# Layer norms as ScalarE activations, retention's moments on VectorE, and a planner that lists single operations

## The chip, the cores and the metric

The kernel runs on one core of a Trainium2 chip. A core has five engines with a queue of instructions each: TensorE (PE) for matrix products, VectorE (DVE), ScalarE (ACT) and GpSimd (POOL) for elementwise work, and SyncE (SP), which here only starts DMAs. SBUF holds the working data in 128 partitions; PSUM takes the results of PE, in banks of 128x512 float32. The metric is device time in microseconds (us).

## The reference, cut to what matters

The input `x` is 4 sequences of 512 tokens with 128 features. Eight sublayers follow each other, each as `x = x + f(layernorm(x))`. The layer norm has no weights:

```python
def _layernorm(x, axis=-1, eps=1e-05):
    m = jnp.mean(x, axis=axis, keepdims=True)
    v = jnp.var(x, axis=axis, keepdims=True)
    return (x - m) / jnp.sqrt(v + eps)
```

The sublayers are, in order: softmax attention with 16 heads of 8; a mixture of 8 experts, top 2; Favor+ linear attention; the experts again; a gated linear attention with 8 heads of 64, which has a layer norm of its own on the normed input and adds that input back (`residual`); a feed-forward of width 352 whose activations and weights are rounded to FP4 in blocks of 16; retention with 16 heads of 8; and the feed-forward again. Retention ends in a norm over all 512 tokens and the 8 features of a head:

```python
mean = y.mean(axis=(1, 3), keepdims=True)      # y: (batch, head, token, feature)
var = y.var(axis=(1, 3), keepdims=True)
y = (y - mean) * jax.lax.rsqrt(var + GN_EPS)
y = y.reshape(B, T, C) * gn_w + gn_b
```

## The kernel before, in words

All of `x` stays in SBUF as `X`, 16 tiles of 128 tokens by 128 features; a batch (one sequence) is four tiles. A norm of a batch has three parts. `moments` (L265) lets DVE take mean and variance of each tile (`bn_stats`, `bn_aggr`). `rstd` (L249) computes 1/sqrt by an integer first guess on DVE and three Newton steps, twelve small operations on POOL (L259 to L262). `centred` (L272) then writes `xn = (X - mean) * r` in four POOL operations of 128x128, one per tile, at L275. PE transposes the four tiles into one PSUM bank (L309) and ACT copies that out (`transposed`, L303). Every sublayer's norm goes this way except attention's: there `norm` (L284) takes the moments of all 16 tiles first, does one `rstd` of 128x16 for all four batches, and its four operations per batch are at L298. There are 36 such groups of four: 4 in attention, 8 in the experts (a unit q is one batch in one of the two expert layers), 4 in Favor+, 4 in the gates of the gated attention and 4 for its residual `res` (L984), and 4 in each of the two feed-forwards and in retention.

The program has four stretches. First X is loaded, attention's batch 0 is normed and projected, and 32 DMAs (SP, 16 for `qc` and 16 for `kc`, L363) spread the heads over the padded tiles `qpad` and `kpad`. Then comes attention, a pipeline over 16 units of four heads: scores (L385 takes maxima), exponentials (L410), values. Then one loop over 64 pairs of a unit q and an expert e, whose order is written out by hand; Favor+ and the gates (`gates`, L826) are generators that move one step at a time between the experts' matmuls. A unit's norm, transposes and routing are placed some steps ahead of its first expert. In an expert, POOL multiplies `h` (L584) and DVE finishes it (L585).

The last stretch, which I call the tail, is `rest` (L1267): five streams per batch, as Python generators. `gated` is the gated attention in chunks (`chunked`, L1005), `first` the first feed-forward, `retention` its matmuls, `leveled` its norm and output projection, `second` the second feed-forward, which stores the batch. The class `Clock` (L126) is a planner that runs while the program is built: each stream yields at the places where PE would have to wait, with an estimated due time; `steps` goes on with the stream that can start earliest, and of equals with the one whose number is higher (gated 150 to 270, first 150, retention 110, leveled 75, second 50). Two feed-forwards may be open at a time and one retention. PE's queue has this order exactly; the other engines' queues come from a scheduler and the places where instructions were issued. PSUM has four slots `bank` of one bank and two slots `pair` of two there, which this planner doesn't count.

In a feed-forward, `fp4_pieces` (L1213) rounds by block: DVE takes block maxima (L1217 to L1220), POOL multiplies by the reciprocal scale (L1225), DVE rounds (`fw`), POOL multiplies back (L1235). The four `gates` products go through ACT's silu (L1312) and a DVE product into KD (L1313); `down` rounds half of the result and, tile by tile, transposes it (L1332), copies it to `hT` on ACT (L1334) and multiplies. In retention, the scores of a group G of four heads go through DVE's `copy_predicated` into `rw` (L1395) and through ACT and POOL (L1397). `values` and `leveled` then read:

```python
nc.scalar.activation(y[:, G, :], po, AF.Copy, accum_out=sums[:, G:G + 1])        # L1426
self.mm(ps, k["avg"], sums)                       # mean over a head, by a matmul
nc.vector.tensor_scalar(gm, ps, -1.0, None, ALU.mult)                            # L1451
nc.scalar.activation(off, y[:, G, :], AF.Square, bias=gm[:, G:G + 1], accum_out=gv[:, G:G + 1])   # L1454
self.mm(ps, k["avg"], gv)                         # variance
nc.scalar.activation(y[:, G, :], y[:, G, :], AF.Identity, scale=ga[:, G:G + 1], bias=gm[:, G:G + 1])  # L1463
```

Of the kernel before, what the change touches and what calls it, by code (L numbers as in the profile page):

```python
# [17 lines left out]
P = 128  # L18
# [12 lines left out]
def _constants():  # L31
# [28 lines left out]
    c["avg"] = np.where((g[:, None] == g[None, :]) & (d[:, None] < DH), 1.0 / (DH * T), 0.0)  # L60
# [64 lines left out]
class Clock:  # L125


    def __init__(self):
        self.free, self.since = collections.defaultdict(float), 0.0
# [5 lines left out]
    def pe(self, us):  # L135
        return self.run("pe", 1.1 * us, self.since)

    def dve(self, us, since):
        return self.run("dve", 1.1 * us, since)

    def act(self, us, since):
        return self.run("act", us, since)

    def pool(self, us, since):
        return self.run("pool", us, since)

    def together(self, work):

        while work:
            a = min(work, key=lambda a: a[0])  # L150
            yield a[0]
            t = next(a[1], None)
            if t is None:
                work.remove(a)
            else:
                a[0] = t or self.free["pe"]

    def steps(self, streams):

        left = {name: [0.0, after, takes, None, gen, far] for name, (after, takes, gen, far) in streams.items()}
        rooms = {"ffn": 2, "retention": 1}
        while left:
            can = []
            for name, a in left.items():
                if a[3] is None:
                    if any(n in left for n in a[1]) or rooms.get(a[2], 1) == 0:
                        continue
                can.append((max(a[0], self.free["pe"]), -a[5], a[0], name))  # L170
            ready, name = min(can)[2:]
            a = left[name]
            self.since = ready
            if a[3] is None:
                a[3] = a[4]()
                if a[2]:
                    rooms[a[2]] -= 1
            t = next(a[3], None)
            if t is None:
                del left[name]  # L180
                if a[2]:
                    rooms[a[2]] += 1
                for other in left.values():
                    if name in other[1]:
                        other[0] = max(other[0], ready)
            else:
                a[0] = t or self.free["pe"]


class Net:  # L190
# [81 lines left out]
    def centred(self, pool, b, mv, r, tag="xn"):  # L272
        xn = self.new(pool, [P, J, P], tag)
        for j in range(J):
            self.nc.gpsimd.tensor_scalar(xn[:, j, :], self.xi(b * J + j), mv[:, j, 0:1], r[:, j:j + 1], ALU.subtract, ALU.mult)  # L275
        return xn

    def normed(self, pool, b, tag="xn"):

        mv = self.new(self.stat, [P, J, 2], "mvb")  # L280
        self.moments(b, mv)
        return self.centred(pool, b, mv, self.rstd(mv[:, :, 1], "rstdb"), tag)

    def norm(self, src):  # L284

        nc = self.nc
        mv = self.new(self.stat, [P, NT, 2], "mv")
        for i in range(NT):
            st = self.new(self.stat, [P, 6], "bn", bufs=4)
            nc.vector.bn_stats(st, src(i))  # L290
            nc.vector.bn_aggr(mv[:, i, :], st)
        r = self.rstd(mv[:, :, 1], "rstd")

        def make(pool, b, tag):
            xn = self.new(pool, [P, J, P], tag)
            for j in range(J):
                i = b * J + j
                nc.gpsimd.tensor_scalar(xn[:, j, :], src(i), mv[:, i, 0:1], r[:, i:i + 1], ALU.subtract, ALU.mult)  # L298
            return xn

        return make

    def transposed(self, pool, xn, tag, scale=None, bias=None, banks=None):  # L303

        nc = self.nc
        out = self.new(pool, [P, T], tag)
        ps = self.bank(pool=banks)
        for j in range(J):
            nc.tensor.transpose(ps[:, j * P:(j + 1) * P], xn[:, j, :], self.ident)  # L309
        if scale is None:  # L310
            nc.scalar.copy(out, ps)
        else:
            nc.scalar.activation(out, ps, AF.Identity, scale=scale, bias=bias)
        return out
# [12 lines left out]
    def attention(self, beside=None):  # L327
# [9 lines left out]
        with ExitStack() as ctx:  # L337
            tp = lambda name, bufs: ctx.enter_context(self.tc.tile_pool(name="a_" + name, bufs=bufs))
            big, mid, pt = tp("big", 1), tp("mid", 2), tp("pt", 3)
            norm = self.norm(self.xi)  # L340
# [14 lines left out]
            def prepare(b):  # L355
                xs = self.transposed(mid, norm(mid, b, "xn"), "xnT")
# [411 lines left out]
    def front(self, out):  # L768
# [6 lines left out]
        with ExitStack() as ctx, ExitStack() as now:  # L775
# [50 lines left out]
            def gates(b, mid, banks=None):  # L826
# [10 lines left out]
                xn = self.centred(mid, b, mv[:, b], r2[:, b])  # L837
# [146 lines left out]
            def project(b, pool, ot):  # L984
                res = self.centred(pool, b, mv[:, b], r1[:, b], "res")
# [19 lines left out]
    def chunked(self, arm, tp, clock, D, KD, fall, same, tri, wq, wv, rn, xs, project):  # L1005
# [13 lines left out]
        def queries(u):  # L1019
# [3 lines left out]
            tt(D[b][:, p, :], ps, D[b][:, p, :], ALU.mult)  # L1023

        def by_token(u):
# [7 lines left out]
            tt(split(V[u]), split(ps), _bc(rn[:, b, :, p, :], DI), ALU.mult)  # L1033

        def keys(u):
# [5 lines left out]
            nc.scalar.copy(K[u], ps)  # L1041

        def states(u):
# [6 lines left out]
            for c in range(J - 1):  # L1050
                f = fall[:, b, p, c:c + 1]
                stt(r[:, c, :], ps[:, c, :], f, same, ALU.mult, ALU.mult)
                if c:
                    stt(r[:, c, :], r[:, c - 1, :], f, r[:, c, :], ALU.mult, ALU.add)

        def scores(u):
# [6 lines left out]
            nc.vector.copy_predicated(flat(ws[u % 3]), _over(tri, 2 * J), ps.rearrange("p h c t -> p (h c) t"))  # L1063

        def values(u):
# [8 lines left out]
            nc.scalar.copy(D[b][:, p, :], po)  # L1074

        def before(u):

            queries(u)
            ready[u] = clock.dve(0.7, clock.pe(0.85))
            yield 0  # L1080
            by_token(u)
            t = clock.dve(0.7, clock.pe(0.85))
            yield 0
            keys(u)
            yield max(t, clock.act(0.5, clock.pe(0.35)))
            states(u)
            ready[u] = max(ready[u], clock.dve(1.7, clock.pe(0.65)))

        ready = {}

        def steps(b):
            if b == 0:
                yield from before(0)
            for u in range(NG * b, NG * (b + 1)):
                yield ready[u]
                scores(u)
                t = clock.dve(1.3, clock.pe(0.9))
                yield 0
                if u + 1 < NG * B:
                    yield from before(u + 1)  # L1100
                yield t
                values(u)
                t = clock.act(0.6, clock.pe(1.6))
            yield t
            ps = project(b, once, D[b])
            yield clock.pe(3.5)
            self.add_x(b, ps)
            yield clock.dve(0.7, clock.since)
# [158 lines left out]
    def rest(self, arm, clock, D, KD, out, gated=None):  # L1267
# [18 lines left out]
        for t in (S, va, *ws):  # L1286
            nc.gpsimd.memset(t, 0.0)

        def ffn(b, store=False):
            h, hq = room(KD[b])[:, :J * FF], room(D[b])[:, :J * FF]  # L1290
            scale = lambda n: [self.new(two, [P, n // BLK], f"{t}{n}") for t in ("sc", "rc")]
            pe, dve, act, pool = clock.pe, clock.dve, clock.act, clock.pool
            xn = self.normed(two, b).rearrange("p j d -> p (j d)")
            yield pool(4.5, dve(1.6, clock.since))
            fp4 = self.fp4_pieces(xn, xn, *scale(T), self.new(two, [P, T], "fw"))
            next(fp4), next(fp4)
            yield pool(1.1, dve(1.3, clock.since))
            for _ in fp4:
                pass
            yield pool(1.3, dve(2.2, clock.since))  # L1300
            xT = self.transposed(two, xn.rearrange("p (j d) -> p j d", d=P), "xT")
            yield act(0.6, pe(0.45))
            half = J * FF // 2
            po = []

            def gates():
                for j in range(J):
                    ps = self.pair()
                    for i in range(2):
                        self.mm(ps[:, i, :FF], xT[:, chunks[j]], wT[:, i * FF:(i + 1) * FF])  # L1310
                    o = h[:, j * FF:(j + 1) * FF]
                    nc.scalar.activation(o, ps[:, 0, :FF], AF.Silu)  # L1312
                    tt(o, o, ps[:, 1, :FF], ALU.mult)  # L1313
                    t = dve(0.5, act(0.5, pe(1.2)))
                    if j % 2:
                        work.append([t, down(j // 2)])
                    yield 0

            def down(i):
                c = slice(i * half, (i + 1) * half)  # L1320
                fp4 = self.fp4_pieces(hq[:, c], h[:, c], *scale(half), self.new(two, [P, half], "fh"))
                next(fp4), next(fp4)
                yield pool(1.4, dve(1.5, clock.since))
                for _ in fp4:
                    pass
                yield pool(1.4, dve(2.8, clock.since))
                po[:] = po or [self.bank()]
                for j in (2 * i, 2 * i + 1):
                    ps = self.bank()
                    for c in range(NF):  # L1330
                        w = min(P, FF - c * P)
# [178 lines left out]
```

## Time and profile before

| | |
|---|---|
| median of 3 runs | 1328.7 us (1327.78 to 1331.3) |
| the profiled execution | 1344.16 us, of which the span of its instructions is 1342.3 |
| busy in the span | PE 80%, DVE 52%, POOL 40%, ACT 33% |
| mean granted clock of PE | 0.855 |
| first score matmul of attention | 39.1 us |
| experts and Favor+ begin | about 392 us |
| the tail | 894 to 1340 us |

A line of groups in the profile reads: source line, engine, operation, out<-in, shapes, count, then busy time in all and mean ns of one, then the idle time of the engine just before such instructions and who ended it. A line of waits reads: who waited, at which line, for which engine's output, then us in total, times, and the longest. The row of digits is the busy share in 40 equal slices of the span, in tenths.

### The profile page before, as it was taken

Reading aid. Unit: us, or ns where it says so; the run is one execution under the profiler, and the core shown is the slowest. Engines: PE = TensorE matmul, PEld = TensorE weight load, DVE = VectorE, ACT = ScalarE, POOL = GpSimd, SP = SyncE. Lnnn points to the kernel's source line nnn. Section 1 sums busy time; section 2 is a strip of 40 time slices with the busy share of each in tenths; the row PEclk is TensorE's granted clock in tenths of the full one; section 3 lists DMA queues with packets and bytes.
Section 4 is the critical chain, followed back from the end, with each engine's and each line's share of the span. In section 5 each row is a group of like instructions: output and inputs, shape, how many; then the busy total and the mean of one; then the engine's idle time right before and its main releaser. Section 6 shows DMA issues by size and latency. Waiting matters only on the chain.

```text
span 1342.3 us, 17500 instructions
## 1 busy us (share of the span) xinstructions
PE 1074.0 (80%) x6608; PEld 648.4 (48%) x6608; DVE 692.7 (52%) x1607; ACT 445.2 (33%) x738; POOL 534.5 (40%) x1038
## 2 busy tenths in 40 slices
PE   2799898999999999898978877489778857667745
PEld 1444444444345546364724334267657745456633
DVE  3344454543456566565547463335666745273443
ACT  1133333334344243434235435321111323324311
POOL 7022323132145262626265465391135155472341
PEclk9588989999899898988788897769889988678776
DMA  3000000000200000000000000000000000000000
GB/s 125 12 17 1 15 2 10 8 1 1 68 1 1 1 0 1 0 1 0 1 0 1 0 0 1 0 22 1 1 1 1 1 1 1 1 1 9 1 16 10
DMA packets 9856, 11.37 MB, mean 8 GB/s; under 512 B 2572, under 2 KB 7820, under 8 KB 9508
## 3 DMA queue, kind: packets, MB, share of 16 engines
q1 hardware_dynamic: 9764, 10.17, 2.8%
q8 instruction: 54, 0.88, 0.3%
q14 instruction: 38, 0.31, 0.1%
HBM read 7.02 MB, written 1.05 MB: 6 GB/s over the span
## 4 chain that ended last, share of the span: by engine, by line
PE 49%; DVE 21%; POOL 18%; ACT 6%; issue 4%; SPq 1%; DMA 1%; POOLq 0%; ACTq 0%; DVEq 0%
PE bank L320 32%; PE pair L320 14%; POOL xn L275 5%; DVE tops L385 2%; DVE h L585 1%; DVE D L1218 1%; POOL rstdbt L259 1%; POOL rstdb L262 1%; POOL rstdbt L260 1%; POOL rstdbt L261 1%; POOL sum L623 1%; POOL h L584 1%; DVE fh L1217 1%; DVE top L674 1%; DVE y L621 1%
## 5 line engine op out<-in xcount | busy, mean ns | idle before, releaser
L385 DVE TENSOR_REDUCE tops<-pair 128x2 f32<-128x256 f32 (+3 forms) x128 | 98.6, 820 | 126.4 <-PE pair L320 126.4
L320 PE MATMUL bank<-xe,we 128*128 128x512 f32 x256 | 140.9, 676 | 4.8 <-DVE h L585 3.6
L410 ACT ACTIVATE w<-pair 128x1024 f32<-128x1024 f32 (+1 forms) x96 | 82.3, 880 | 152.2 <-PE pair L320 151.9
L412 POOL TENSOR_SCALAR_AFFINE_SELECT w<-w 128x256 f32<-128x256 f32 x128 | 50.2, 406 | 195.1 <-ACT w L410 194.4
L623 POOL TENSOR_TENSOR sum<-sum,y 128x512 f32<-128x512 f32 x56 | 71.1, 1269 | 109.6 <-DVE y L621 59.4
L320 PE MATMUL pair<-qm,kpad 32*128 32x256 f32 (+3 forms) x512 | 93.5, 520 | 15.6 <-DVE tops L385 9.3
L309 PE MATMUL bank<-ident,xn 128*128 128x128 f32 x128 | 32.4, 347 | 62.8 <-POOL xn L275 34.4
L320 PE MATMUL bank<-h,we 128*128 128x512 f32 x128 | 73.8, 661 | 7.8 <-DVE h L585 6.6
L585 DVE SCALAR_TENSOR_TENSOR h<-bank,ws,h 128x512 f32<-128x512 f32 x52 | 38.8, 746 | 75.7 <-POOL h L584 75.7
L320 PEld LDWEIGHTS bank<-xe,we 128*128 128x128 f32 x256 | 47.3, 206 | 61.3 <-issue 42.8
L275 POOL TENSOR_SCALAR xn<-X,mvb,rstdb 128x128 f32<-128x128 f32 x96 | 74.9, 792 | 2.4
L584 POOL TENSOR_SCALAR h<-h 128x512 f32<-128x512 f32 x64 | 40.7, 637 | 82.8 <-ACT h L583 82.5
L320 PE MATMUL pair<-kpad,qpad 32*128 32x512 f32 (+3 forms) x512 | 65.0, 538 | 10.3 <-DMA kpad<-kc 10.3
L583 ACT ACTIVATE h<-bank,half 128x512 f32<-128x512 f32 x52 | 35.7, 687 | 103.4 <-PE bank L320 103.4
L320 PE MATMUL pair<-fwT,xT 128*128 128x352 f32 x128 | 53.1, 557 | 17.4 <-DVE KD L1313 9.9
L320 PEld LDWEIGHTS pair<-qm,kpad 32*128 32x128 f32 x512 | 39.6, 203 | 51.9 <-DVE tops L385 24.7
L320 PE MATMUL bank<-xs,wg 128*128 128x512 f32 x96 | 58.2, 706 | 4.5 <-DVE k L1366 2.9
L601 DVE TENSOR_TENSOR xe<-xnT,bank 128x512 f32<-128x512 f32 x64 | 43.3, 677 | 32.3 <-PE bank L320 32.0
L309 PEld LDWEIGHTS bank<-ident,xn 128*128 128x128 f32 x128 | 18.7, 165 | 83.4 <-POOL xn L275 44.5
L621 DVE SCALAR_TENSOR_TENSOR y<-bank,ws,x 128x512 f32<-128x512 f32 x56 | 41.7, 744 | 28.1 <-PE bank L320 28.1
L1225 POOL TENSOR_TENSOR D<-KD,rc 128x704 f32<-128x704 f32 x16 | 24.5, 1532 | 70.5 <-ACT KD L1312 27.5
L320 PE MATMUL bank<-w,vpad 128*32 128x128 f32 (+3 forms) x512 | 52.0, 469 | 0.0
(314 smaller groups left out, 2311.3 us busy)
## 6 DMA issues: line engine op xcount, KB each, us to landing
we<-in_we_dram SPq DMA_DIRECT2D x1, 1536.0 KB
wg<-in_wg_dram SPq DMA_DIRECT2D x1, 1280.0 KB
X<-in_x_dram SPq DMA_DIRECT2D x4, 256.0 KB
qpad<-qc SPq DMA_DIRECT2D x64, 16.0 KB
kpad<-kc SPq DMA_DIRECT2D x64, 16.0 KB
out_dram<-X SPq DMA_DIRECT2D x4, 256.0 KB
wf<-in_wf_dram SPq DMA_DIRECT2D x1, 560.0 KB
wb<-in_wb_dram SPq DMA_DIRECT2D x1, 512.0 KB
```

The source lines that it names most:

```text
L275: self.nc.gpsimd.tensor_scalar(xn[:, j, :], self.xi(b * J + j), mv[:, j, 0:1], r[:, j:j + 1], ALU.subtract, ALU.mult)
L309: nc.tensor.transpose(ps[:, j * P:(j + 1) * P], xn[:, j, :], self.ident)
L320: self.nc.tensor.matmul(out, lhsT=lhsT, rhs=rhs, start=start, stop=stop)
L385: nc.vector.tensor_reduce(top[:, c, :].rearrange("p (i r) -> p i r", r=32)[:, 2 * h:2 * h + 2, DH], pp[h][:, :, o:o + (c + 1) * P], AX.X, ...
L410: nc.scalar.activation(w[:, :, :end], pp[h][:, :, :end], AF.Exp, scale=scale)
L412: nc.gpsimd.affine_select(out=w[:, :, o:o + P], in_=w[:, :, o:o + P], pattern=[[0, 2], [1, P]], compare_op=ALU.is_ge, fill=0.0, base=0, ch ...
L583: nc.scalar.activation(h, p, AF.Tanh, scale=0.5, bias=hb)
L584: nc.gpsimd.tensor_scalar(h, h, 0.5, 0.5, ALU.mult, ALU.add)
L585: stt(h, p, b, h, ALU.add, ALU.mult)
L601: tt(xe, xnT[q], ps, ALU.mult)
L621: stt(y, ps, b2[:, e:e + 1], x3, ALU.add, ALU.mult)
L623: nc.gpsimd.tensor_tensor(sums[q], sums[q], y, ALU.add)
```

## The change

`centred` leaves two small operations on POOL, the offset `-mean * r` of the four tiles, and does the norm itself as four ACT activations with a scale and a bias per partition. Attention's own `norm` is removed, and each of its batches takes moments and `rstd` for itself. In retention the plain ACT copy has no accumulator; DVE takes `bn_stats` and `bn_aggr` of each group's y. `leveled` averages the means over a head, adds the squared distance of each mean to the variances in four small DVE operations, and averages that; the final scaling of y goes to DVE for even G, and stays on ACT for odd G. The planner no longer lengthens PE's and DVE's durations by 1.1, keeps a list of single operations of all engines and issues each at its planned time among the streams (`later`), counts the slots of PSUM, and lets a stream say what it needs: operations and slots. Several durations and the numbers of two streams change, and the down projections are issued as turn, turn, down, down instead of turn, down, turn, down.

```diff
-    def centred(self, pool, b, mv, r, tag="xn"):
-        xn = self.new(pool, [P, J, P], tag)
+    def centred(self, xn, b, mv, r):
+        off = self.new(self.stat, [P, J], "off")
+        self.nc.gpsimd.tensor_tensor(off, mv[:, :, 0], r, ALU.mult)
+        self.nc.gpsimd.tensor_scalar(off, off, -1.0, None, ALU.mult)
         for j in range(J):
-            self.nc.gpsimd.tensor_scalar(xn[:, j, :], self.xi(b * J + j), mv[:, j, 0:1], r[:, j:j + 1], ALU.subtract, ALU.mult)
+            self.nc.scalar.activation(xn[:, j, :], self.xi(b * J + j), AF.Identity, scale=r[:, j:j + 1], bias=off[:, j:j + 1])
         return xn
...
             def prepare(b):
-                xs = self.transposed(mid, norm(mid, b, "xn"), "xnT")
+                xs = self.transposed(mid, self.normed(mid, b), "xnT")
...
-                nc.scalar.activation(y[:, G, :], po, AF.Copy, accum_out=sums[:, G:G + 1])
-                return act(0.8, pe(2.3))
+                def stats():
+                    st = self.new(two, [P, 6], "gst")
+                    nc.vector.bn_stats(st, y[:, G, :])
+                    nc.vector.bn_aggr(mv[:, G, :], st)
+
+                ended.append(later("dve", 0.75, later("act", 0.6, pe(2.0), lambda: nc.scalar.copy(y[:, G, :], po), "bank"), stats))
...
-            for G in range(NG):
-                nc.scalar.activation(off, y[:, G, :], AF.Square, bias=gm[:, G:G + 1], accum_out=gv[:, G:G + 1])
+            self.mm(ps, k["avg"], mv[:, :, 0])
+            def around():
+                nc.vector.tensor_scalar(gm, ps, -1.0, None, ALU.mult)
+                tt(gv, mv[:, :, 0], gm, ALU.add)
+                tt(gv, gv, gv, ALU.mult)
+                tt(gv, gv, mv[:, :, 1], ALU.add)
...
+            def level(G):
+                if G % 2:
+                    nc.scalar.activation(y[:, G, :], y[:, G, :], AF.Identity, scale=ga[:, G:G + 1], bias=gm[:, G:G + 1])
+                else:
+                    nc.vector.tensor_scalar(y[:, G, :], y[:, G, :], ga[:, G:G + 1], gm[:, G:G + 1], ALU.mult, ALU.add)
...
-            streams[f"retention{b}"] = ([f"first{b}"], "retention", lambda b=b: retention(b), 110)
-            streams[f"leveled{b}"] = ([f"retention{b}"], None, lambda b=b: leveled(b), 75)
+            streams[f"retention{b}"] = ([f"first{b}"], "retention", lambda b=b: retention(b), 205)
+            streams[f"leveled{b}"] = ([f"retention{b}"], None, lambda b=b: leveled(b), 170)
```

In the planner, the loop that picks the next step now chooses among operations and streams together, an operation coming first where the times are equal:

```diff
     def pe(self, us):
-        return self.run("pe", 1.1 * us, self.since)
+        return self.run("pe", us, self.since)
...
+    def later(self, engine, us, after, do=None, gives=None):
+        op = SimpleNamespace(engine=engine, us=us, after=after, do=do, gives=gives, end=None)
+        self.ops.append(op)
+        return op
...
+            for op in self.ops:
+                t = self.when(op.after)
+                if t is not None:
+                    can.append((max(t, self.free[op.engine]), -1000, len(can), t, op))
...
+                kinds = collections.Counter(a.needs[1:])
+                t = max([t] + [sorted(self.slots[kind])[n - 1] for kind, n in kinds.items()])
+                can.append((max(t, self.free["pe"]), -a.far, len(can), t, name))
```

## The prediction

> **What bounds the kernel now.** I read the page first: busy shares, the slices and the chain of work that ended last.
>
> ```profile
> PE 1074.0 (80%) x6608; PEld 648.4 (48%) x6608; DVE 692.7 (52%) x1607; ACT 445.2 (33%) x738; POOL 534.5 (40%) x1038
> PE   2799898999999999898978877489778857667745
> PEclk9588989999899898988788897769889988678776
> ...
> PE 49%; DVE 21%; POOL 18%; ACT 6%; issue 4%; SPq 1%; DMA 1%; POOLq 0%; ACTq 0%; DVEq 0%
> ```
>
> PE is the bound in the middle (slices at 8 and 9), but not at the start (first slice 2), around slice 26 (a 4) and in the last third (5 to 7 with a lower clock). There the chain runs over DVE and POOL: POOL holds 18% of the chain with 40% busy, ACT 6% with 33%. So work that leaves POOL for ACT leaves a chained engine for one with room. Next, the groups of POOL, ACT and DVE, where the operations that move are priced:
>
> ```profile
> L275 POOL TENSOR_SCALAR xn<-X,mvb,rstdb 128x128 f32<-128x128 f32 x96 | 74.9, 792 | 2.4
> L1463 ACT ACTIVATE D<-D,gm,ga 128x512 f32<-128x512 f32 x16 | 11.7, 802 | 8.1 <-POOL gm L1461 8.1
> L1454 ACT ACTIVATE off<-D,gm 128x512 f32<-128x512 f32 x16 | 11.6, 723 | 3.2 <-DVE gm L1451 3.0
> ```
>
> Then PE's waits by stretch. From the experts to the gates of the second layer (392 to 877 us), and in the tail (894 to 1340), the columns being total, times, longest:
>
> ```profile
> PE bank L309 <- POOL xn L275: 34.4, 32, 7.0
> PE bank L320 <- DVE h L585: 13.9, 4, 6.6
> ```
> ```profile
> PE bank L1332 <- POOL D L1235: 13.8, 3, 8.6
> PE pair L320 <- DVE rw L1395: 13.4, 6, 4.6
> PE pair L320 <- DVE KD L1313: 12.5, 5, 4.4
> PE bank L320 <- ACT off L1454: 10.1, 4, 3.1
> ...
> PE bank L320 <- DVE rw L1395: 9.9, 1, 9.9
> ```
>
> All waits of the tail add to about 110 us of 446, scattered over ten causes; only the ACT one (Square passes) is removed outright. Last, the chain of the tail in order of time: eleven lumps "POOL xn L275 x4" of 3.1 us each lie on it, and four "ACT D L1463 x4" of 2.93.
>
> [...] a POOL multiply of the experts whose input was ready at 605.7 ran at 612.9, behind a norm.[...] The trace shows 0.50 from 877 to 894, after PE idled from 864 to 877.[...]
>
> **Part 1, the norm itself.** Before: four POOL subtract-multiplies at 792 ns, pitch 780, so 3.12 us a group; 36 groups (144 instructions, 112.3 us of POOL). After: two dependent POOL operations on 128x4 (pitch 280 ns from the rstd rows: 0.56),[...] and four ACT Identity with two pointers on 128 elements. None is in the trace[...]. A group takes 2.2 to 2.3 instead of 3.12: **−0.8 to −1.0 where it is on the path**.[...] POOL sheds 112−20 = 92 us[...].
>
> *Attention* (39 to 392): norms of later batches run far ahead of PE; 0, cover is the banded work. Bound ±2: four ACT groups and four rstd chains stand among exponentials and evictions there.
>
> *Experts and favor:* eight expert norms have PE's transposes waiting for them (the 34.4, with gates): 8·0.8 = −6.5. POOL's multiply h no longer stands behind 3.1 us of norm, so part of the 13.9 goes: −2. Against it, the order of the instructions has one place (about 397 us) where ACT has favor's first norm ahead of the copy of the third expert batch's transposes; its offset comes from POOL about 4.5 us later than that copy was due: +5. Net **−3** (−12 to +6). The gates' serial stretch 842 to 877: −1.
>
> **Part 2, attention's norm by batch.** The first batch now waits for 4 tiles of statistics, not 16: bn+aggr at 271+167 ns ends about 4 us sooner, but the chain is then on POOL, whose memsets last to 15.75 before and after; rstd's 12 operations ended at 19.0. Now two rstd chains interleave on POOL (28 operations at 0.22 to 0.28, against 12), and ACT's order is: batch 0, batch 1, the copy, batch 1, three of batch 2, and only then the eviction qc. Batch 2's offset needs its rstd from POOL after those two chains. qc heads 16 DMA issues of 0.67 us on SP and the 10.3 us that PE waits for kpad; SP's order itself doesn't change. I estimate qc at 28.3 in place of 25.5: **+3** (0 to +6).
>
> **Part 3, retention's moments.** Per retention batch: four ACT evictions lose the accumulator (597+194 to 585 ns), four Squares (723+189 each, 3.65 us of chain) go. Added on DVE: 4·(0.7+0.17) = 3.5 us; statistics of 512 elements are not in the trace, and 0.7 is an estimate: 271 ns for 128 elements (L269) and 384 more at 1.14 ns, the slope between DVE's rows of 352 and 704 elements (L1313 519, L1218 920); bounds 0.5 to 1.0. Three of four lie beside later values; only the last, 0.87, is on the path, with three more tiny DVE operations (0.5). Net −2.2 each, and PE now has a neighbour's gate matmuls between the two averages: 4·2.2 **≈ −9** (all of 10.1 is in the waits). Levels: 2 on ACT, 2 on DVE, 1.5 instead of 2.93; silus no longer queue behind four: part of the 12.5 wait on KD, **≈ −4**.
>
> **Part 4, the account.** Single operations are queued by start time, PSUM's slots are counted, and retention and leveled get higher numbers than the gates of feed-forward. Instructions and DMAs are the same; PE's order changes from the tail's start only. The down projections go in pairs: turn, turn, down, down, which hides the hT copies (6.9, 13 times): **−2**. Otherwise what is worth counting is part 1's norm on the tail's chain: eleven lumps, of which all but the 9.9 case's two are worth 0.9: **−8**; the 9.9 wait (DVE's rw stands behind fp4's fw, this behind POOL's multiply, this behind two norms at 1087.5 and 1092.8) loses two lumps of 3.1 from POOL: **−5**. Against all this: ACT now takes 16 tail groups ahead of hT, rw, kt and y evictions: 16·0.5 = **+8**; DVE gets 19 us more (statistics 16·0.87 = 13.9, eight levels at 0.4, an estimate, 3.2, small ones 2) in 446 of which it is busy over half; I charge a fifth of it where it delays mask selections: **+4**. Sum −9−4−2−8−5+8+4 = −16; the clock, 0.61 to 0.78 from 1100 on, returns some of the idle time removed: −4. Tail **−20** (−50 to +20).
>
> **Sum**: +3 +0 −3 −1 −20 = −21 against the profiled execution's 1344.2 us (span 1342.3 and 1.9 around it): 1323. This execution is 15.5 us (1.2%) above the median of the three runs, 1328.7; I take the same difference off that: **1308**.
>
> **Rivals.** (A) As summed, about 1308, own range 1280 to 1323: chance 0.65. (B) Slower: ACT as a queue. An activation at the head that waits for POOL's offset stops every PSUM eviction behind it, thus PE; POOL's norm never did that. For: the two places found in the order (qc at the start, the transposes at 397), together +8; ACT owns hT, xT, kt, y and half the scores in the tail. Against: ACT is 33% busy. The forecast's gains add to 41.5 us; less start and DVE (3+4) 34.5 stand against 36 groups, so it decides once a group holds back something that PE needs for 34.5/36 = 0.96 us on average; the forecast charges 13/36 = 0.36. With 1.25 us: 45−34.5 = +10, 1339. Chance 0.18. (C) Nothing: DVE, in the tail's chain with 21%, takes statistics and levels in front of copy_predicated (1288 ns), and what POOL gives back DVE takes: charge two thirds of 19 instead of a fifth (+9) and lose the −8 of the lumps: −21+9+8 = −4, 1325, within 4 of 1328.7, chance 0.07. The change doing nothing to the order is excluded, as it moves 144 instructions. (D) Better: the four long waits (8.6, 9.9, 7.6, 7.1) vanish with POOL's relief and the new order[...]: −45, 1284, chance 0.10.
>
> A measurement tells about 0.3% (4 us) from no change. Faster: A, D and no part of B: 0.75; same 0.07; slower 0.18. Range 1277 to 1336 leaves out B's upper half and D's lower.
>
> **What would show it.** Four xn activations on ACT in 1.6 us with a POOL row of two small operations; first pair matmul at 42 rather than 39.1; PE's wait for xn from 392 to 877 falling from 34 to 28 but a new wait for xnT or h near 400; no wait on off, instead a small one on DVE's gst; PE's slices in the last third at 7 to 8. Wrong if PE waits on ACT xn, xT or hT add over 25 us in the tail, or bn_stats of 512 costs over 1 us.

## Result, and the profile after

The changed kernel takes 1316.23 us (median of 6 runs, 1311.47 to 1318.63) against 1330.0 for the kernel before (6 runs, 1325.49 to 1332.77): a ratio of 0.9895 with a 95% interval of 0.9869 to 0.9922, so 13.8 us or 1.05% faster. Forecast were 1308 us, 1277 to 1336, and 21 us less. Its profiled execution has a span of 1314.1 us at a mean clock of 0.868.

The page of the changed kernel, the same lines as were shown of before:

```profile
PE 1059.8 (81%) x6608; PEld 636.3 (48%) x6608; DVE 725.9 (55%) x1668; ACT 478.1 (36%) x826; POOL 441.5 (34%) x1002
PE   1789787998898989898996888739797796777764
PEclk9689698888998999899988888867998898898876
...
PE 48%; DVE 25%; POOL 13%; ACT 7%; issue 5%; SPq 1%; DMA 0%; ACTq 0%; POOLq 0%; DVEq 0%
```

POOL fell by 93 us busy (92 were forecast) and from 18% to 13% of the chain. What POOL gave up on the chain went to DVE, 21% to 25%, more than to ACT, 6% to 7%. The last third of PE's slices is denser, but there is a second new thing: in slices 5 to 10, in attention, PE's clock reads 6 9 8 8 8 8 where it read 9 8 9 9 9 9, and there the forecast expected nothing.

The groups of ACT and of DVE:

```profile
L296 ACT ACTIVATE xn<-X,off,rstdb 128x128 f32<-128x128 f32 x96 | 40.1, 483 | 88.2 <-POOL off L294 88.2
```
```profile
L1474 DVE BATCH_NORM_STATS2 gst<-D 128x6 f32<-128x512 f32 x16 | 11.1, 692 | 11.8 <-ACT D L1477 11.8
L1526 DVE TENSOR_SCALAR D<-D,ga,gm 128x512 f32<-128x512 f32 x8 | 5.1, 657 | 13.6 <-POOL gm L1518 13.6
```

The prices held. The norm's activation took 483 ns; the trace of before has none, and an estimate from its rows gives 500: the 802 of L1463, which also has a scale and a bias per partition, less the 302 by which a copy of 512 elements (L473, 585) is longer than one of 128 (L706, 283). The statistics took 692 (0.7 us). Only DVE's level came at 657 ns instead of 0.4 us; the trace of before has a like `TENSOR_SCALAR` of 128x512, with constants, at 417 (`fw<-fw`, L1217). But the first line has more in it than a price: the idle time ahead of these ACT instructions is 88.2 us, and it ended with POOL's offset. What stood behind them in ACT's queue waited too: in the rows at 138 us below, a copy ready from 138.1 ran at 142.48.

To see where the time went I cut each trace at four instructions of PE that every kernel here has: the first score matmul (`pair<-kpad,qpad`), the first expert matmul (`bank<-xe,we`), the `onesp` product after the gates, and the end. The windows from these cuts, kernel before first, then a second profile of it (experiment 10), then the changed kernel; the columns are the stretch, its length, busy time (instructions) of PE, PEld, DVE, ACT and POOL, the mean clock, and the DMA's share and rate. These borders are not those used above: attention ends here at 348.9 us, where the table ahead of the prediction has the experts begin at about 392, and the tail begins at 877.4 instead of 894.

```profile
39.10:348.90 309.80, 278.33 (x2093) 134.51 (x2093) 141.50 (x283) 108.19 (x144) 75.89 (x192) 0.88 0.06 14
348.90:877.40 528.50, 445.60 (x1598) 239.76 (x1597) 294.14 (x709) 208.06 (x318) 243.63 (x463) 0.87 0.00 1
877.40:1342.30 464.90, 342.66 (x2902) 270.33 (x2902) 245.04 (x568) 125.09 (x271) 189.45 (x345) 0.81 0.02 5
```
```profile
38.00:340.00 302.00, 268.79 (x2094) 129.33 (x2095) 141.62 (x283) 108.18 (x144) 75.85 (x192) 0.92 0.06 15
340.00:859.20 519.20, 440.22 (x1599) 235.96 (x1599) 294.13 (x709) 208.21 (x319) 243.67 (x463) 0.88 0.00 1
859.20:1325.40 466.20, 347.62 (x2902) 274.42 (x2900) 245.38 (x568) 125.07 (x271) 189.93 (x345) 0.81 0.02 5
```
```profile
39.50:366.10 326.60, 286.40 (x2093) 136.46 (x2093) 142.53 (x293) 114.41 (x160) 67.59 (x196) 0.86 0.06 13
366.10:882.75 516.65, 441.27 (x1599) 237.07 (x1599) 296.07 (x709) 225.14 (x371) 208.56 (x437) 0.88 0.00 1
882.75:1314.10 431.35, 325.93 (x2902) 259.94 (x2902) 273.56 (x620) 130.24 (x279) 144.43 (x313) 0.86 0.02 5
```

The tail repeats within 1.3 us between the two profiles of before, and in the changed kernel it is 34 us shorter: 16.7 of it (against the first profile) is PE's busy time, 342.7 to 325.9, the same matmuls at a clock of 0.86 instead of 0.81; the rest is idle time of PE, which is the length less the busy time. Attention is **17 to 25 us longer**. Experts with gates differ by 9 us between two profiles of one kernel; against the second one the change is −2.6. A gain of 34 and a loss of about 20 make the 13.8.

PE's waits: first for xnT in attention in the kernel before, then those of the changed kernel in attention, from the experts to the gates, and in the tail:

```profile
PE bank L320 <- ACT xnT L311: 2.3, 3, 0.8
```
```profile
PE bank L326 <- ACT xnT L317: 10.1, 3, 5.0
...
PE pair L326 <- ACT w L415: 2.5, 3, 1.6
```
```profile
PE bank L308 <- ACT xn L296: 27.8, 8, 7.2
...
PE bank L326 <- ACT xnT L317: 4.8, 2, 3.6
```
```profile
PE bank L1353 <- POOL D L1239: 23.5, 7, 8.6
PE pair L326 <- DVE rw L1441: 20.5, 8, 7.6
PE bank L308 <- POOL xn L1239: 15.1, 2, 7.8
```

In the experts both signs came as forecast: 27.8 instead of 34.4 for xn, and a new 3.6 us wait for xnT, at 421 us. In the tail no wait on the Squares is left; FP4's chains through POOL and the mask selections have grown into the largest, and PE waits 9.6 us for copies of xnT where it waited 0.7. The timeline says what happens in attention. Columns: start, duration, engine, instruction, and in brackets the idle time ahead and what ended it.

```profile
137.82 0.27 PE L308 MATMUL bank<-ident,xn 128*128 128x128 f32 x1
138.26 1.65 ACT L296 ACTIVATE xn<-X,off,rstdb 128x128 f32<-128x128 f32 x4 [8.55 <-POOL off L294]
139.81 1.91 ACT L415 ACTIVATE w<-pair 128x1024 f32<-128x1024 f32 x2
...
142.08 0.49 ACT L296 ACTIVATE xn<-X,off,rstdb 128x128 f32<-128x128 f32 x1 [0.36 <-POOL off L294]
142.48 0.56 ACT L317 COPY xnT<-bank 128x512 f32<-128x512 f32 x1
...
143.09 2.08 PE L326 MATMUL bank<-xnT,wa 128*128 128x512 f32 x2 [5.00 <-ACT xnT L317]
```

The first row is the last of four transposes on PE: from 138.1 us on, the copy xnT, which belongs to attention's batch 2, had all that it needs. It only stood in ACT's queue behind two norms of others. The first xn belongs to the experts' norm of batch 0: its statistics could only start when attention's output had been added to X (131.4 us), and POOL's chain gave the offset at 138.2. ACT stood 8.55 us for it, with exponentials and the copy xnT behind it. The second xn is attention's norm of batch 3 (those of batches 0 to 2 were done by 27 us), whose `rstd` ran on POOL behind that of the experts. PE idled 5.0 us, and the clock record shows half speed from 140.5 on, for 20.5 us. At 225 us the experts' next norm holds ACT again, 4.89 us for its offset, and PE waits 4.3 us for batch 3's xnT; there no second norm stands in between.

### The profile page after: what moved, and what is told of

Read it like the earlier page. It is cut to its first block, busy times and chain, and to the rows that moved or that the text cites. A ratio compares the mean times of both kernels' runs of the same rounds, so it can differ in the third digit from the quotient of the medians.

```text
span 1314.1 us, 17607 instructions
## 1 busy us (share of the span) xinstructions
PE 1059.8 (81%) x6608; PEld 636.3 (48%) x6608; DVE 725.9 (55%) x1668; ACT 478.1 (36%) x826; POOL 441.5 (34%) x1002
## 3 DMA queue, kind: packets, MB, share of 16 engines
HBM read 7.02 MB, written 1.05 MB: 6 GB/s over the span
## 4 chain that ended last, share of the span: by engine, by line
PE 48%; DVE 25%; POOL 13%; ACT 7%; issue 5%; SPq 1%; DMA 0%; ACTq 0%; POOLq 0%; DVEq 0%
PE bank L326 30%; PE pair L326 14%; DVE tops L390 2%; ACT xn L296 2%; DVE D L1222 2%; POOL rstdb L281 2%; POOL rstdbt L278 2%; POOL rstdbt L279 2%; POOL rstdbt L280 2%; DVE h L590 1%; DVE top L679 1%; DVE fh L1221 1%; PE bank L308 1%; DVE bn L288 1%; DVE y L626 1%
## 5 line engine op out<-in xcount | busy, mean ns | idle before, releaser
L326 PE MATMUL pair<-kpad,qpad 32*128 32x512 f32 (+3 forms) x512 | 68.9, 561 | 13.8 <-DMA kpad<-kc 11.9
L308 PE MATMUL bank<-ident,xn 128*128 128x128 f32 x112 | 27.5, 348 | 62.5 <-ACT xn L296 47.0
L296 ACT ACTIVATE xn<-X,off,rstdb 128x128 f32<-128x128 f32 x96 | 40.1, 483 | 88.2 <-POOL off L294 88.2
L326 PE MATMUL pair<-fwT,xT 128*128 128x352 f32 x128 | 50.3, 534 | 17.0 <-DVE rw L1441 12.9
L590 DVE SCALAR_TENSOR_TENSOR h<-bank,ws,h 128x512 f32<-128x512 f32 x52 | 38.8, 747 | 36.4 <-POOL h L589 36.4
L278 POOL TENSOR_TENSOR rstdbt<-rstdb 128x4 f32<-128x4 f32 x108 | 22.1, 206 | 98.6 <-DVE rstdb L276 92.7
L308 PEld LDWEIGHTS bank<-ident,xn 128*128 128x128 f32 x112 | 16.0, 162 | 79.9 <-ACT xn L296 56.6
```

The costliest lines, as they stand in the source:

```text
L278: tt(t, r, r, ALU.mult)
L296: self.nc.scalar.activation(xn[:, j, :], self.xi(b * J + j), AF.Identity, scale=r[:, j:j + 1], bias=off[:, j:j + 1])
L308: self.nc.tensor.transpose(ps[:, j * P:(j + 1) * P], xn[:, j, :], self.ident)
L326: self.nc.tensor.matmul(out, lhsT=lhsT, rhs=rhs, start=start, stop=stop)
L590: stt(h, p, b, h, ALU.add, ALU.mult)
```

## Experiments

The kernels were cut at the same four instructions. In brackets stand two times in us: "half" adds up the stretches at half clock, by the clock record, that began in the stage, each to its end (one already running at the stage's start is left out; at attention's start that is up to 46 us), and "idle" is PE's idle time. Each ratio is to runs of the kernel before on the same chip in the same round of runs, so kernels are better compared by ratios than by medians.

| kernel | median us | ratio to before (95%) | attention (half; idle) | experts + gates | tail (half; idle) |
|---|---|---|---|---|---|
| before | 1330.0 | 1 | 309.8 (44; 31.5) | 528.5 | 464.9 (158; 122.2) |
| before, second profile | | | 302.0 (21; 33.2) | 519.2 | 466.2 (157; 118.6) |
| changed | 1316.2 | 0.9895 (0.9869–0.9922) | 326.6 (75; 40.2) | 516.6 | 431.4 (104; 105.4) |
| 1 all_pool | 1323.0 | 0.9888 (0.984–0.9935) | 315.0 (58; 31.8) | 519.2 | 448.1 (118; 122.4) |
| 2 act_only | 1347.5 | 1.0091 (1.0034–1.0149) | 335.0 (72; 39.6) | 521.4 | 459.5 (139; 116.6) |
| 3 q_pool | 1311.6 | 0.9824 (0.9781–0.9866) | 318.7 (58; 38.1) | 518.4 | 431.5 (104; 105.7) |
| 4 one_norm | 1314.2 | 0.9856 (0.9803–0.9908) | 326.7 (72; 38.8) | 516.6 | 431.7 (104; 105.7) |
| 5 q_pool_one | 1301.6 | 0.978 (0.9727–0.9834) | 307.5 (44; 32.7) | 524.1 | 431.6 (108; 106.5) |
| 6 mom_act | 1318.8 | 0.9896 (0.9846–0.9947) | 327.7 (85; 39.8) | 518.3 | 432.2 (112; 106.6) |
| 7 old_numbers | 1326.1 | 0.9974 (0.9944–1.0005) | 322.3 (65; 40.4) | 516.6 | 445.0 (121; 111.4) |
| 8 unpaired | 1326.0 | 0.9951 (0.9917–0.9986) | 326.2 (68; 39.7) | 517.9 | 439.7 (126; 106.5) |
| 9 pool_planned | 1327.9 | 0.9949 (0.9922–0.9976) | 317.4 (41; 33.0) | 519.1 | 454.9 (132; 122.0) |
| 11 mom_dve | 1344.0 | 1.0076 (1.0052–1.01) | 311.6 (51; 31.6) | 518.9 | 476.4 (160; 133.9) |

Several rows share a stage, and so show how far it repeats. The attention of the kernel before stands in three profiles (both of before and 11): 302.0 to 311.6 us, idle 31.5 to 33.2. That of the changed kernel stands in four (changed, 6, 7 and 8): 322.3 to 327.7 us, idle 39.7 to 40.4. The idle time is thus the sharper measure. The changed kernel's tail stands in four (changed, 3, 4 and 5) and repeats within 0.3 us.

**1 all_pool.** The norm back on POOL in the changed kernel.

```diff
-        off = ...                      # two POOL operations
-            self.nc.scalar.activation(xn[:, j, :], ..., AF.Identity, scale=r[:, j:j + 1], bias=off[:, j:j + 1])
+            self.nc.gpsimd.tensor_scalar(xn[:, j, :], ..., mv[:, j, 0:1], r[:, j:j + 1], ALU.subtract, ALU.mult)
```

> The changed kernel with the norm's four operations back on POOL (no offset operations); statistics by batch, retention's moments and the planner stay. Theory 1 (the +17 us that attention lost comes from ACT's queue: a norm at its head that waits for POOL's offset holds the exponentials and the copy of xnT): attention, from the first pair matmul to the first expert matmul, takes 309 to 314 us instead of 326.6, while the experts, from there to the onesp matmul, go back to 526 to 530 instead of 516.7 and the tail loses 5 to 10 of the 33 us it won: in all 1307 to 1316. Theory 2 (attention's loss is an accident of where the half-clock windows fell): attention stays anywhere between 310 and 327 with PE waiting for xnT under 3 us in both, and the total is about 1316 plus 15.

Attention gets 11.6 us shorter (315.0, a microsecond over what was expected), the tail 16.7 longer (5 to 10 were expected), and the ratio is that of the changed kernel: moving the norm to ACT bought nothing that these runs can tell as a whole, since it gave back in attention what it won in the tail. PE's wait for xnT in attention is the old one:

```profile
PE bank L323 <- ACT xnT L314: 2.2, 3, 0.8
```

PE's idle time in attention is also that of before (31.8), so statistics by batch (part 2) cost no waiting while the norms are on POOL. What makes 315.0 longer than before's 302 to 312 is PE's busy time; why it is longer is not shown. In the tail PE is busy as long as in the changed kernel and idle as long as before: there ACT's norm saves waiting.

**2 act_only.** The norm on ACT in the kernel before, nothing else (attention's one norm kept, with one pair of offset operations).

```diff
+        off = self.new(self.stat, [P, J], "off")       # off = -mean * r, two POOL operations
-            self.nc.gpsimd.tensor_scalar(xn[:, j, :], self.xi(b * J + j), mv[:, j, 0:1], r[:, j:j + 1], ALU.subtract, ALU.mult)
+            self.nc.scalar.activation(xn[:, j, :], self.xi(b * J + j), AF.Identity, scale=r[:, j:j + 1], bias=off[:, j:j + 1])
```

> The kernel before with nothing but the norm on ACT (two offset operations on POOL, four activations); attention keeps its one rstd for all four batches. Theory 1: attention loses 5 to 15 us already here, by the experts' norms that are issued beside it, as these wait at ACT's head; experts gain 8 to 11; the tail gains 8 to 12 (eleven lumps of 3.1 us on its chain shrink by about 0.9): 1318 to 1330. Theory 2: attention as before (310 us) and the whole is 1308 to 1312.

The title's first part alone makes the kernel **slower**, by 0.9%, which neither theory expected. Attention takes 335.0 us, more than the 5 to 15 expected. That length is on the high side: the profiled execution was the slowest of the four (1356.4 us), with 46 us of half clock left over from before attention. But PE's idle time, 39.6 us, is that of the changed kernel. The tail gains only about 6 (459.5 against 464.9 and 466.2; 8 to 12 were expected), and PE's wait for hT there grows from 6.9 to 16.0 us. In attention it has the wait of the changed kernel:

```profile
PE bank L326 <- ACT xnT L317: 8.9, 3, 4.5
...
PE pair L326 <- ACT w L416: 3.4, 3, 2.5
```

**3 q_pool.** In the changed kernel the experts' norms that are issued beside attention go to POOL.

```diff
+                    self.on_pool = True
                     for do in todo[step]:
                         do()
+                    self.on_pool = False
```

> The changed kernel, but the three experts' norms that are issued while attention runs stay on POOL; all others on ACT. Theory 1: PE's waits for xnT in attention (10.1 us) fall under 4, the half-clock windows behind them go, attention takes 310 to 316 us instead of 326.6, the total is 1302 to 1309. Theory 2: no difference beyond 4 us, 1312 to 1320. A third possibility, that the statistics of attention's own batches (part 2) hold xnT, keeps the wait at xnT and gives 1312 to 1316 too, but with ACT idle ahead of xnT.

A part of the loss goes (318.7), but PE's idle time in attention hardly falls (38.1), and one of its three waits for xnT grew to 6.7 us. The timeline shows the third possibility:

```profile
145.67 0.49 ACT L302 ACTIVATE xn<-X,off,rstdb 128x128 f32<-128x128 f32 x1 [6.38 <-POOL off L300]
146.07 0.56 ACT L323 COPY xnT<-bank 128x512 f32<-128x512 f32 x1
```

ACT now takes its exponentials in time and stands idle for the offset of attention's batch 3, whose chain on POOL began at 141.76, behind the experts' `rstd` and norm.

**4 one_norm.** In the changed kernel attention has one `rstd` and one pair of offset operations for all four batches again, on ACT.

```diff
-                xs = self.transposed(mid, self.normed(mid, b), "xnT")
+                xs = self.transposed(mid, one_norm(b), "xnT")     # statistics, rstd and off of 16 tiles, made once
```

> The changed kernel, but attention takes the statistics of all 16 tiles and one rstd and one pair of offset operations for all four batches first, as the kernel before did, with the norms on ACT. Theory 1 with the blame on the experts' norms alone: attention keeps most of its loss, total 1311 to 1318. If it is attention's own chain of statistics (bn, 12 POOL operations, two offsets, about 7 us, then xn) that is late behind add_x: attention takes 312 to 318 us and the total falls to 1303 to 1309. The start: qc comes at about 24 us instead of 25.9, so the first pair matmul at 38 instead of 39.5.

Attention keeps all of its length (326.7; PE's waits for xnT add to 8.3 us): now the experts' norm at ACT's head holds everything alone. The start came as expected, the first score matmul at 38.3 us. Neither cure is enough by itself.

**5 q_pool_one.** Both edits of 3 and 4.

> The changed kernel with both attention edits together: experts' norms that run beside attention on POOL, and attention's own norm with one rstd for all batches (still ACT). Theory: two causes hold xnT, a norm at ACT's head that waits for the expert chain, and the batch's own chain that queues behind that one on POOL; only taking away both frees it. Attention 308 to 313 us against 326.6, PE's wait for xnT under 3, tail unchanged at 431 to 432; total 1296 to 1303. Rival: the loss sits in clock windows and not in these waits: attention stays above 318 and the total at 1310 or more.

Attention falls to 307.5 us, inside the two profiles of before, the tail stays, and PE's wait for xnT is the old one:

```profile
PE bank L332 <- ACT xnT L323: 2.3, 3, 0.8
```

PE's idle time is that of before too (32.7). The two waits are thus the cause, one behind the other. The lower clock goes with them: "half" is 44 us here and 21 to 51 in the three profiles of before's attention, but 65 to 85 in the four of the changed one. This is the fastest kernel of the study, 1301.6 us; its interval, 0.9727 to 0.9834, lies below that of the changed kernel.

**6 mom_act.** Retention's moments and all four levels back on ACT in the changed kernel, the planner told.

```diff
-                ended.append(later("dve", 0.75, later("act", 0.6, ...copy...), stats))
+                ended.append(later("act", 0.8, ..., AF.Copy, accum_out=mv[:, G:G + 1]))
+            yield later("act", 3.65, later("dve", 0.3, ...gm...), squares), "bank"
```

> The changed kernel with retention's moments (accumulating evictions, four Squares) and all four levels back on ACT; the planner has them as ACT operations of 0.8, 3.65 and 0.75 us. By the prediction's step for part 3 the tail gets 9 + 4 = 13 us longer: 444 instead of 431.4, total about 1329. Rival: DVE, the busiest engine of the tail after PE, is relieved of 19 us, and the planner fills the Squares with other streams' matmuls: tail 430 to 436.

The tail is 0.8 us longer, not 13, though DVE is busy there for 250.6 us instead of 273.6. Part 3 brings next to nothing here.

**7 old_numbers** (retention 110 and leveled 75 in place of 205 and 170) and **8 unpaired** (turn, down, turn, down):

```diff
-            streams[f"retention{b}"] = (..., lambda b=b: retention(b), 205)
-            streams[f"leveled{b}"] = (..., lambda b=b: leveled(b), 170)
+            streams[f"retention{b}"] = (..., lambda b=b: retention(b), 110)
+            streams[f"leveled{b}"] = (..., lambda b=b: leveled(b), 75)
```
```diff
-                turns = []
                 for j in (2 * i, 2 * i + 1):
                     yield halves[i], "bank"
-                    turns.append(turn(j))
-                for j in (2 * i, 2 * i + 1):
-                    hT, op = turns[j % 2]
+                    hT, op = turn(j)
```

> The changed kernel with the streams' numbers as before (retention 110, leveled 75). If the numbers carry the planner's gain, the tail gets 6 to 16 us longer (438 to 447) because retention's long chain again starts behind gates; if the gain comes from listing single operations and from the norms, the tail stays within 3 us of 431.4.

> The changed kernel with the down projections in the old turn, down, turn, down order; the rest of the planner stays. By the prediction's step the hT waits of 6.9 us come back in part: the tail is 2 to 5 us longer (433 to 436). Rival: the planner places other streams between turn and down, so nothing: 430 to 432.

The tail takes 13.6 and 8.3 us more. With the old numbers the gated attention ends sooner, 157.5 us from its first to its last score matmul instead of 174.6, and what is left after it takes 266.5 instead of 235.8. That retention's chains then come too late to be covered is argued from this, not shown. Of the 13.6 us, 6.0 are idle time of PE. Unpaired (2 to 5 us were expected), PE's wait for hT grows; the changed kernel first:

```profile
PE bank L326 <- ACT hT L1357: 0.4, 2, 0.2
```
```profile
PE bank L326 <- ACT hT L1357: 14.1, 18, 3.4
```

Yet PE's idle time in the whole tail grows only from 105.4 to 106.5 us: other waits shrank, on rw from 20.5 to 16.2 and on xnT from 9.6 to 2.7. Most of the 8.3 us is PE's busy time, 333.2 instead of 325.9 on the same matmuls. So the pairs' order is worth 8.3 us, but that it is so through the waits for hT is not shown.

**9 pool_planned.** As all_pool, with the planner's durations for it.

```diff
-            return xn, later("act", 1.2, op, lambda: ...)
+            return xn, later("pool", 3.1, op, lambda: ...)
```

> The changed kernel with all norms on POOL, and the planner told so (3.1 us on POOL for a norm and for res, where it had 1.2 on ACT). If ACT's shorter norm itself made the 16.7 us by which the tail of all_pool is longer than that of the changed kernel, the tail stays at 442 to 448 us. If the plan that believed in ACT made them, the tail returns to 431 to 438. Attention 315 (as in all_pool).

454.9 us, longer than with the plan that believed in ACT (448.1), and above both expectations. So ACT's norm is worth 17 to 24 us in the tail under the new planner, and a truer account of the norm did not give a better order. As in experiment 1, PE's idle time in the tail (122.0) is that of before.

**10 before_again.** The kernel before, unchanged.

> The kernel before, profiled a second time, to see how far a stage of it repeats: if stages repeat as the tails of the changed kernel and its attention variants did, attention is 309 to 311 us, experts with gates 526 to 531 and the tail 463 to 467; where the clock's half windows fall otherwise, experts with gates may be as short as 520.

The tail repeats (466.2), attention and experts do not: 302.0 against 309.8, 519.2 against 528.5, with PE busy 9.5 and 5.4 us less. Experiment 11, which leaves both stages as they were, has 311.6 and 518.9. A stage's difference below 10 us in attention or experts cannot be read from one pair of profiles.

**11 mom_dve.** Retention's moments on DVE, levels shared, in the kernel before with its old planner, which has the durations of the new operations.

```diff
-                nc.scalar.activation(y[:, G, :], po, AF.Copy, accum_out=sums[:, G:G + 1])
+                nc.scalar.copy(y[:, G, :], po)
+                nc.vector.bn_stats(st, y[:, G, :])
+                nc.vector.bn_aggr(sums[:, G, :], st)
...
-                nc.scalar.activation(off, y[:, G, :], AF.Square, bias=gm[:, G:G + 1], accum_out=gv[:, G:G + 1])
...
+                nc.vector.tensor_scalar(y[:, G, :], y[:, G, :], ga[:, G:G + 1], gm[:, G:G + 1], ALU.mult, ALU.add)   # even G
```

> The kernel before with retention's moments on DVE and levels shared by DVE and ACT, in the old planner; nothing else. If the prediction's price of part 3 was right for the old order (10.1 us of waits on off go), the tail falls by 6 to 13 us from 464.9, to 452 to 459. If DVE's 19 us take the place, it stays within 3 us, 462 to 468. Attention and experts as before.

Slower than before, by 0.8%; the tail is 10.2 to 11.5 us longer, outside both expectations. The Squares' wait of 10.1 us is gone, but:

```profile
PE pair L320 <- DVE rw L1395: 29.1, 10, 8.5
...
PE bank L320 <- DVE D L1469: 18.7, 4, 7.3
```

PE waits 29.1 us for retention's mask selections (13.4 before) and 18.7 for the levels on DVE. DVE is busy for 22.1 us more in the tail (267.1 against 245.0). That the selections stand behind DVE's new work, and the levels behind selections and FP4 of other streams, is a reading of the queues that no run tests.

## Why the prediction was right in time and wrong in its parts

The direction and the range held, and the forecast missed by 8 us. Its terms held less well:

- **The price of the norm** held: a group of four took 1.65 us on ACT and 2.19 with its two offset operations (137.72 to 139.91 us; 2.2 to 2.3 were forecast), and POOL was relieved by what was worked out. What the forecast put in for the four activations was not shown by any trace. The estimate from rows of before gives 1.72 us: four times 500 ns, less the 278 by which four L1463 in a row (2.93 us) are shorter than 4·802.
- **Start, +3**: mis-sized, and +0.4 against the first profile. qc came at 25.87 instead of 25.46, the first score matmul at 39.5 against 39.1 and 38.0 in the two profiles of before. ACT did hold qc for batch 2's offset, but that came at 24.7, sooner than was reckoned.
- **Attention, 0 ("cover is the banded work")**: the step that failed. What was measured is +17 to +25 us, and +18 between the means of the three and the four profiles. The prediction had the four ACT groups standing among exponentials and evictions in the order, and priced them by their duration only; it did not ask when the offset of each would come. The three experts' norms that also run beside attention (on POOL at 142.9, 217.4 and 292.2 us in the kernel before) it counted with the experts alone. That question was asked at 397 us and at the start, where it found 5 and 3 us. It is rival B's mechanism, at a place that rival B did not name. Experiments 3 to 5 show it by taking away either wait and both.
- **Experts and gates, −4**: −2.6 against the second profile of before. The first pair of profiles would have said −12; experiments 10 and 11 (519.2 and 518.9) show that most of that is spread.
- **Part 3, −13**: wrong. Taken back in the changed kernel it is worth 0.8 us (experiment 6), and done alone it costs 10.2 to 11.5 (experiment 11). The wait on off was real and went; the mis-sized term is DVE's, +4 for the whole tail. The added busy time was near, 22 to 23 us (experiments 11 and 6) instead of 19, but a fifth of it was charged: done alone, with the wait of 10.1 us gone and the tail 10.2 to 11.5 us longer, it cost about 20 (an estimate from these figures), nearly all of it.
- **Part 4, −2**: mis-sized. The streams' numbers alone carry 13.6 us and the pairs 8.3, by taking each back. The prediction took the planner's order as given and priced only the hT copies, at 2 of 6.9 us; what the numbers of the streams do to PE's order it put at nothing.
- **The norm in the tail, −8 −5 +8**: −5 as summed, and −6 in the old order (experiment 2). In the new order it is worth 17 to 24 (experiments 1 and 9). The parts are not additive: taken back one by one they make 0.8 + 13.6 + 8.3 + 16.7 = 39, and the tail's gain is 34.
- **The clock, −4**: PE's busy time in the tail fell by 16.7 us on the same matmuls, and grew by 8 to 18 in attention. The −4 was the author's estimate, and how much clock a given idle time costs was not shown. Three stretches at half clock can be read. In attention it set in at 140.5 us, at the end of 3.4 us in which PE was busy for 0.96, and full clock came at 161.0, after PE had worked without a gap from 150.8. Another stretch, from 130.3, lasts only 3.4 us, with PE busy for all of it, so no rule is read from these. In the prediction's own example, whose 0.50 is PE's clock, it reads 0.59 over 868 to 872 and 0.50 over 872 to 877, while PE idles, and 0.50 in the next 17 us, in which PE was busy for 16.56:

```profile
877.00:894.00 17.00, 16.56 (x52) 11.91 (x53) 3.80 (x9) 6.52 (x10) 15.23 (x17) 0.50 0.15 44
```

- **What would show it wrong**: PE's waits on xT and hT in the tail are 1.3 and 0.4 us, 11.3 with the 9.6 of the like copy xnT, and statistics of 512 elements cost 0.69, so neither sign came; the signs looked at the tail, and the loss was in attention. Of rival C, the half that has DVE's statistics and levels ahead of the mask selections fits what part 3 does alone; POOL gives nothing back there.
- **A sum**: the waits of the tail that the prediction read as about 110 us add to 117.6; no term rests on it.

Two large errors of opposite sign, some 20 us in attention and 14 in the tail, nearly cancelled. The forecast was near by luck, for other reasons than it gave. What stays open is how the 17 us of ACT's norm in the new tail divide between the shorter chain and the DVE and POOL work that moves up with it, and by which waits the new order of the streams and the pairs shortens the tail; no run here separates these.

## What to carry to other kernels

In these runs, work moved to an engine with room (ACT, 33% busy before) cost more than its duration where its inputs were not there when it reached the head of that engine's queue: at 138.26 us four activations took 1.65 us, and ACT had stood 8.55 for their offset. A copy ready from 138.1 waited behind two norms that it had no use for and ran at 142.48; so for every moved instruction look up in the order what stands behind it, and in the trace when its last input comes. A pipeline's stages can each be priced from two profiles of the same kernel, not one; here two profiles of the kernel before differed by 8 and 9 us in two stages while the third stood still. PE's idle time in a stage repeated better than the stage's length. Before crediting a part of a change with its gain, do it alone and take it back alone: here the norms on ACT and the moments on DVE each made the kernel before slower, and the norms pay in one stage only, the tail: about 6 us there in the old order of PE's work, 17 to 24 in the new one.

## What the runs showed of the hardware that was not expected

The loss in attention is larger than the waiting in it. Between the means of before's three profiles and the changed attention's four it is 17.9 us (307.8 to 325.7): 7.9 are idle time of PE (32.1 to 40.0), and 10.0 are the same matmuls taking longer. And the place of the half-clock stretches is not fixed by the program: the same instructions of attention ran for 72 us at half clock in one profile of the kernel before and for 48 in the other, counting only the time inside the stage.
